# A graph and feed-forward network on one core: where 480 block-table scatters are issued

## The chip, the cores and the metric

The kernel runs on one core of one Trainium2 chip, as one program. The metric is the device time of one execution in microseconds; of the kernel before there are three timed runs, given by their median, and one further execution that was profiled. Engines are named PE (TensorE), DVE (VectorE), ACT (ScalarE), POOL (GpSimd) and SP (SyncE, which here only issues DMAs).

## The reference

Four layers, each a graph step over the same 60,000 edges followed by a feed-forward step over the 3,750 nodes of width 256, each added to the node features `x`:

```
edge_index = jnp.stack([src, dst])
x = x + _L0_gnn_ref(_layernorm(x), ..., src, dst, edge_type_8)
x = x + _L0_ffn_ref(_layernorm(x)[None], ...)[0]
x = x + _L1_gnn_ref(_layernorm(x), ..., edge_index)
x = x + _L1_ffn_ref(_layernorm(x)[None], ...)[0]
x = x + _L2_gnn_ref(_layernorm(x), edge_index, ...)
x = x + _L2_ffn_ref(_layernorm(x)[None], ...)[0]
x = x + _L3_gnn_ref(_layernorm(x), edge_index, ...)
x = x + _L3_ffn_ref(_layernorm(x)[None], ...)[0]
```

The graph steps of layers 0 to 2 are attentions: each edge gets a logit from its two nodes, the logits are put through a softmax over the edges with the same destination, and the source rows are summed with these weights. Layer 3's graph step is a sum over the edges in one direction and back in the other:

```
m = segment_sum(xt[src], dst) * Binv[:, None]
out = segment_sum(m[dst], src) * Dinv[:, None]
```

No number of the result depends on when the block table, of which the change speaks, is written, as long as it is whole before layer 3's blocks are made from it.

## The kernel before

**Staging.** The edges are sorted by destination; the node rows lie in 30 tiles of 128. A program for regular inputs (class `Regular`) runs the phases one after the other: layer 0's features, then `l01` (layers 0 and 1), layer 2, layer 3.

**An attention step** (`Regular.attention`, from line 1844) runs over 75 groups of 7 chunks of 128 edges. For each chunk POOL issues one indirect DMA (`gather`, line 149) that brings 128 rows of the layer's node table from DRAM into the tile `gt`; that makes 525 gathers for a layer. The gathers of group g+1 are issued ahead of the work on group g. PE selects the destination's part of the logits (`ad_ps`, line 1129 in layer 1), DVE adds the gathered part (line 1136), every few groups a softmax over 112 rows is made, and PE sums the weighted rows into `sum_ps` (line 1965). The instructions of DVE, PE, ACT and POOL keep the order in which this loop writes them.

**The node table** of each layer is written just before: in layer 1 (`l1_gnn`, line 1081) for each of the 30 tiles PE multiplies the normed rows with the weights, ACT copies the product (`h`), and SP stores it to DRAM (`l1_h`, line 1111; profile names leave the digits out, so it is `l_h` there). Layer 2 does the same with `l2_vk` (line 1314, `l_vk` in the profile), which its gathers read. A gather waits for all 30 stores of its table. Layer 0's table, `l_feat`, was made earlier, before `l01`.

**The block table.** Layer 3 works with dense blocks of the graph. They are made, during layer 2's feed-forward, from a DRAM table `blocks` that says for every place which edge sits there. It is filled by 480 scatters, each an indirect DMA on POOL (`scatter`, line 154) that writes one four-byte entry for each of 125 rows to a place of its own; the places and entries were worked out beforehand and lie in `put_dram`. The scatters are declared independent of each other.

**Where the scatters are.** `l01` (line 2028) issues them in two trains, each after an attention step has been issued in full and before the feed-forward step of the same layer. POOL works off its queue in order, so a train follows the 525 gathers of its own layer and stands ahead of the gathers of the next. Neither feed-forward step gives POOL any work. The helper `beside` does one train: it reserves the tile `put`, has DVE clear it near the end of the attention (the hook `self.behind`, called when the last group's gathers are out), which keeps the load of `put` from going ahead of its time, loads `put` by a DMA on POOL's queue (line 2047), and issues the scatters one column at a time. The tiles of both trains, `put0` and the second, lie beside each other in one pool, and hold 480 columns between them.

Of the kernel before, what the change touches and what calls it, by code (L numbers as in the profile page):

```python
# [28 lines left out]
EP, EC = 125, 480  # L29
# [29 lines left out]
class Gnn:  # L59
# [938 lines left out]
    def l01(self):  # L998
        self.l0_gnn()
        self.sort_by_src(self.l0_ffn)  # L1000
        self.l1_gnn()
        self.l1_ffn()
# [814 lines left out]
class Regular(Gnn):  # L1817
# [210 lines left out]
    def l01(self):  # L2028


        nc = self.nc
        self.blocks = self.dram.tile([P * NCB, 1], I32, name="blocks")
        with ExitStack() as st:
            with ExitStack() as st2:
                wp, = self.pools(st2, none=1)
                none = wp.tile([P, NCB], I32, name="none")
                nc.gpsimd.memset(none, P)
                nc.sync.dma_start(self.blocks.rearrange("(p k) a -> p (k a)", p=P), none)
            pool, = self.pools(st, put=1)
            group = self.new_group()  # L2040

            def beside(gnn, c0, c1):
                put = pool.tile([EP, 2, c1 - c0], I32, name=f"put{c0}")

                self.behind = lambda: nc.vector.memset(put, 0)
                gnn()
                nc.gpsimd.dma_start(put, self.put_dram[:, :, c0:c1])
                for c in range(c1 - c0):
                    self.scatter(self.blocks, put[:, 0, c:c + 1], put[:, 1, c:c + 1], group)
            beside(self.l0_gnn, 0, 320)  # L2050
            self.l0_ffn()
            beside(self.l1_gnn, 320, EC)
            self.l1_ffn()
            self.behind = None

# [255 lines left out]
```

## Time and profile before

| | |
|---|---|
| timed runs, us | 6545.5, 6604.4, 6623.24 (median 6604.4) |
| the profiled execution's own time, us | 6483.59 |
| its span, us | 6481.8 |
| busy PE, DVE, ACT, POOL, us | 4548.9, 3065.8, 2065.1, 2916.3 |
| mean granted TensorE clock | 0.80 |
| scatters | 480, of 1.17 us at least, 1.18 in the median, 44.98 at most |
| first and last start of a scatter, us | 1185.9, 2792.4 |
| gathers of layer 0, first and last start, us | 366.7, 1157.9 |
| gathers of layer 1 | 525, from 1690.0 to 2482.1 |
| gathers of layer 2 | 525, from 2975.5 to 3875.8 |
| first read of `blocks` | 3906.8 |

All times within the execution are counted from the start of its span. "Busy" counts work on the engine itself; register, branch, semaphore and DMA-issuing instructions aren't in it. For a gather or a scatter on POOL the trace shows the interval in which POOL works on the instruction, with some 0.30 us between one and the next. [...] a line of the profile gives, next to an instruction, how long its engine sat idle before it and what released it; "issue" there means that it waited for nothing that the profile shows.

### The profile page before, as it was taken

What the parts mean: (1) busy time and instruction counts of PE and PEld (TensorE: products, weight loads), DVE (VectorE), ACT (ScalarE), POOL (GpSimd) and SP (SyncE); (2) the same over time, 40 slices, a digit from 0 to 9 for tenths busy, and PEclk for the clock granted to TensorE, in tenths of its full rate; (3) what the DMA queues carried; (4) which work ended last, traced back from release to release, by engine and by line L of the source; (5) the groups of instructions that cost most, each with busy time, mean ns of one, the idle gap of its engine ahead of it and who ended that gap; (6) DMA issues with size and microseconds to landing.
All of it is one profiled execution on the core that took longest, in us unless ns stands there. A gap on an engine that the chain in (4) does not pass through costs nothing. (4 is left out here: it accounts for less than half of the span.)

```text
span 6481.8 us, 64863 instructions
## 1 busy us (share of the span) xinstructions
PE 4548.9 (70%) x20438; PEld 3297.5 (51%) x20438; DVE 3065.8 (47%) x7333; ACT 2065.1 (32%) x4862; POOL 2916.3 (45%) x2845
## 2 busy tenths in 40 slices
PE   6826666695066664896566773798879898896885
PEld 3425555464055553554454662576546565564673
DVE  5634443793033336544566777403532342266435
ACT  1125554322055553322444552222631121110121
POOL 0046666677766666713455650012025445452124
PEclk9957777797577776898777885697589999998896
DMA  4334444102244442114555661222434554455114
GB/s 148 133 97 116 116 117 116 40 2 42 57 114 117 114 118 63 16 47 148 163 169 163 202 199 43 95 85 77 160 126 143 136 133 131 134 147 160 50 55 116
DMA packets 431163, 714.02 MB, mean 110 GB/s; under 512 B 117452, under 2 KB 308628, under 8 KB 426716
## 3 DMA queue, kind: packets, MB, share of 16 engines
q0 software_dynamic: 145136, 379.81, 22.7%
q1 hardware_dynamic: 267064, 316.47, 15.5%
q10 hardware_dynamic: 18612, 13.50, 0.7%
q8 instruction: 166, 2.72, 0.2%
q14 instruction: 185, 1.52, 0.1%
HBM read 583.81 MB, written 125.15 MB: 109 GB/s over the span
## 5 line engine op out<-in xcount | busy, mean ns | idle before, releaser
L1965 PE MATMUL sum_ps<-gt,oh 128*128 128x260 f32 (+2 forms) x3150 | 1016.4, 483 | 355.9 <-issue 187.4
L1965 PEld LDWEIGHTS sum_ps<-gt,oh 128*128 128x128 f32 x3150 | 744.0, 243 | 551.7 <-issue 226.6
L150 POOL DMA_INDIRECT gt<-l_vk,srci x525 | 497.2, 947 | 586.1 <-issue 186.6
L156 POOL DMA_INDIRECT blocks<-put x480 | 644.5, 1343 | 154.1 <-issue 145.7
L150 POOL DMA_INDIRECT gt<-l_feat,g x525 | 501.1, 954 | 304.4 <-issue 242.1
L150 POOL DMA_INDIRECT gt<-l_h,srci x525 | 496.5, 946 | 296.8 <-issue 203.5
L1947 DVE TENSOR_TENSOR gt<-gt,bank 128x1792 f32<-128x1792 f32 x225 | 453.4, 2015 | 111.1 <-issue 60.8
L1839 ACT ACTIVATE oh<-iota,dloc 128x128 f32<-128x128 f32 x1575 | 481.4, 386 | 32.4 <-PE sum_ps L1965 19.5
L150 POOL DMA_INDIRECT gt<-l_mtab,l_idxm x300 | 294.5, 982 | 361.1 <-ACT gt L2170 208.5
L150 POOL DMA_INDIRECT gt<-l_xtab,srci x262 | 254.2, 970 | 389.7 <-DMA l_xtab<-xt 192.6
L2184 PE MATMUL two_ps<-l_twox,slab 128*128 128x512 bf16 x1080 | 370.1, 391 | 26.7 <-issue 26.6
L147 PE MATMUL y_ps<-f_w,hT 128*128 128x256 f32 x1600 | 357.8, 383 | 17.0 <-DVE y L1075 16.8
L2184 PE MATMUL two_ps<-l_twom,slab 128*128 128x512 bf16 x1080 | 359.8, 379 | 0.0
L2184 PEld LDWEIGHTS <-slab 128*128 128x128 bf16 x2160 | 213.4, 99 | 271.8 <-issue 44.4
L147 PEld LDWEIGHTS y_ps<-f_w,hT 128*128 128x128 f32 x1600 | 305.7, 192 | 68.2 <-DVE y L1075 21.7
L2186 PE MATMUL third_ps<-l_thirdx,slab 128*128 128x257 bf16 x1080 | 300.0, 279 | 23.4 <-issue 19.5
L1830 ACT ACTIVATE ohT<-rows,iota_p 128x896 f32<-128x896 bf16 x225 | 235.2, 1045 | 249.1 <-issue 139.3
L2186 PE MATMUL third_ps<-gt,oh 128*128 128x257 f32 x1124 | 273.9, 388 | 35.4 <-DVE oh L2173 29.6
L2186 PE MATMUL third_ps<-l_thirdm,slab 128*128 128x257 bf16 x1080 | 294.8, 273 | 0.0
L1922 ACT ACTIVATE fw<-fw 112x128 f32<-112x128 f32 x76 | 23.5, 309 | 827.6 <-DVE fw L1921 546.9
L1129 PE MATMUL ad_ps<-l_node,ohT 128*128 128x4 f32 x1050 | 151.2, 269 | 187.5 <-DVE l L1136 134.1
L1322 PE MATMUL q_ps<-l_qt,ohT 128*128 128x256 f32 x1050 | 251.6, 393 | 39.9 <-DVE gt L1328 30.3
(544 smaller groups left out, 8689.5 us busy)
## 6 DMA issues: line engine op xcount, KB each, us to landing
rows<-dl_dram SPq DMA_DIRECT2D x225, 224.0 KB
slab<-adT SPq DMA_DIRECT2D x36, 960.0 KB
slab<-ad SPq DMA_DIRECT2D x30, 1152.0 KB
l_feat<-ft SPq DMA_DIRECT2D x30, 1040.0 KB
f_w<-in_L_ffn_w_dram SPq DMA_DIRECT2D x18, 1024.0 KB
adT<-db_rowT SPq DMA_DIRECT2D x36, 480.0 KB
ad<-db_row SPq DMA_DIRECT2D x36, 480.0 KB
f_yt<-y SPq DMA_DIRECT2D x114, 128.0 KB
```

The source lines that it names most:

```text
L147: self.nc.tensor.matmul(ps, xT[:, c, :], w[:, c, :], start=(c == 0), stop=(c == kc - 1))
L150: return self.nc.gpsimd.indirect_dma_start(out=out, out_offset=None, in_=table, in_offset=bass.IndirectOffsetOnAxis(ap=idx, axis=0))
L156: inst = self.nc.gpsimd.indirect_dma_start(out=table, out_offset=bass.IndirectOffsetOnAxis(ap=idx, axis=0), in_=src, in_offset=None)
L1129: nc.tensor.matmul(ps[:, j, :], ohT[:, j * P:(j + 1) * P], node[:, ds(tiles[j], 1), :H].rearrange("p a h -> p (a h)"), start=True, stop=True)
L1322: nc.tensor.matmul(ps[:, j, :], ohT[:, j * P:(j + 1) * P], flat(q[:, ds(tiles[j], 1), :]), start=True, stop=True)
L1830: nc.scalar.activation(t, rows, AF.Abs, bias=self.iota_p, scale=-1.0)
L1839: nc.scalar.activation(oh[:, j, :], self.iota, AF.Abs, bias=self.dloc[:, c + j:c + j + 1], scale=-1.0)
L1922: nc.scalar.activation(fw, fw, AF.Exp)
L1947: nc.vector.tensor_tensor(rows, rows, wj.unsqueeze(3).to_broadcast([P, GC, H, DH]), ALU.mult)
L1965: nc.tensor.matmul(open_[1], oh[:, j, :], gt[:, j, :W], start=starts(k), stop=starts(k + 1))
L2184: nc.tensor.matmul(flat(ps), block, flat(two[n][:, blocks[i][1]]), start=(i == 0), stop=(i == len(blocks) - 1))
L2186: nc.tensor.matmul(ps3[:, :D + 1], block, rhs, start=(i == 0), stop=(i == len(all3) - 1))
```

## The change

The border between the two trains moves from column 320 to column 215. The first train, behind layer 0's attention, then has 215 scatters in place of 320, and the second, behind layer 1's, has 265 in place of 160. Nothing else is edited; which scatters there are, what each writes and the order among them stay as they were.

```
-            beside(self.l0_gnn, 0, 320)
+            beside(self.l0_gnn, 0, 215)
             self.l0_ffn()
-            beside(self.l1_gnn, 320, EC)
+            beside(self.l1_gnn, 215, EC)
             self.l1_ffn()
             self.behind = None
```

`EC` is 480. On the engines' queues the changed program differs in this alone: the column counts of the two `put` tiles, of their clears on DVE and of their loads on POOL, and the place of 105 scatters on POOL, which go from ahead of layer 1's 525 gathers to behind them. PE, ACT and SP issue the same instructions in the same order.

## The prediction

> **What bounds the kernel now.** I began with the page: no engine is busy for more than 70% of the span (PE), and the chain of waits that ended last is only followed back to 3674 us, so it says nothing of layers 0 and 1, where the change lies. I therefore read the scatters themselves (tile `blocks`): 480 of them on POOL, from 1185.9 to 2792.4 us, in two trains. Then the table of stretches, cut at the end of layer 0's feed-forward, at the last store of layer 1's table and at the end of the first train. Its columns are the stretch, its length, busy time of PE, PE weight loads, DVE, ACT and POOL with instruction counts, granted TensorE clock, DMA share and GB/s:
>
> ```profile
> 1520.00:1565.00 45.00, 39.45 (x188) 30.91 (x188) 17.28 (x82) 21.74 (x89) 35.86 (x31) 0.96 0.38 95
> 1565.00:1690.00 125.00, 1.85 (x9) 1.76 (x9) 0.00 (x0) 3.10 (x3) 99.12 (x85) 0.50 0.10 6
> 1690.00:1750.00 60.00, 12.85 (x59) 12.64 (x59) 2.88 (x13) 5.45 (x5) 45.46 (x48) 0.50 0.42 112
> ```
>
> In the middle row only POOL works: 85 scatters, while PE has 1.85 us of work in 125, DVE none. The waits of this part and the timelines around it say who waits for what (start, length, engine, line; in brackets idle before and releaser):
>
> ```profile
> DVE l L1136 <- DMA gt<-l_h,srci: 146.9, 2, 138.2
> ...
> 1532.55 1.18 POOL L156 DMA_INDIRECT blocks<-put  x1 [0.30 <-issue]
> 1534.03 1.18 POOL L156 DMA_INDIRECT blocks<-put  x1 [0.30 <-issue]
> ...
> 1561.93 0.32 SPq L1111 DMA_DIRECT2D l_h<-h  x1
> ...
> 1688.53 1.18 POOL L156 DMA_INDIRECT blocks<-put  x1 [0.30 <-issue]
> 1690.02 1.00 POOL L150 DMA_INDIRECT gt<-l_h,srci  x1 [0.30 <-issue]
> ...
> 1700.59 0.19 DVE L1136 TENSOR_TENSOR l<-ad_ps,gt 128x28 f32<-128x28 f32 x1 [138.23 <-DMA gt<-l_h,srci]
> ```
>
> The table that layer 1 gathers from gets its last store at 1561.93, but the first gather stands in POOL's queue behind the 320th scatter and goes out at 1690.02, with the usual 0.30 us of issue before it: it waited for its turn, not for data. DVE waits 138 us for its rows, and PE and ACT wait for DVE. So the time here is set by POOL's queue. At the other end of layer 1 it is the reverse:
>
> ```profile
> 2792.35 1.18 POOL L156 DMA_INDIRECT blocks<-put  x1 [0.30 <-issue]
> 2975.52 1.05 POOL L150 DMA_INDIRECT gt<-l_vk,srci  x1 [181.99 <-DVE hd_hc L702]
> ```
>
> The second train (160) is over 182 us before layer 2's first gather, which is held by the table: DVE starts the attention's constants at 2974.88, released by the landing of `l_vk`. PE is busy 107.86 of 115 us in the stretch 2860 to 2975, so the wait there is real work.
>
> [...] DVE gets its rows at 1700.59. Hence I count POOL's instruction intervals for the queue, and landings apart. [...] two scatters that ran beside unbroken DVE work on two SBUF inputs and ended with it:
>
> ```profile
> 1211.47 27.85 POOL L156 DMA_INDIRECT blocks<-put  x1 [0.30 <-issue]
> ...
> 2540.35 44.98 POOL L156 DMA_INDIRECT blocks<-put  x1 [0.30 <-issue]
> ```
>
> [...] 0.50 granted in the idle stretch, 0.50 in the start after it. So the idle time saves up no clock that its removal would cost.
>
> **The change part by part.** Nothing is added or removed: 480 scatters, two loads of `put`, two DVE clears of `put` (0.59 and 0.33 us for 640 and 320 columns, which become 430 and 530), and the same total of columns. The order of PE, DVE, ACT and SP is unchanged; on POOL 105 scatters move from ahead of layer 1's 525 gathers to behind them. Each carries one DMA of 125 four-byte rows. No queue but POOL's is crossed, and no wait is added.
>
> *First train.* One scatter takes 1.18 us and 0.30 of issue, 1.483 from start to start. The 105 that leave are 105 x 1.483 = 155.7 us. Counted back from the first gather, 1690.02 - 155.7 = 1534.3; the row at 1534.03 is the 216th, so the new train is over at about 1533.7. Its 27.85 us stall is near its start and stays. The table is not there before its last store lands: for `l_vk` the last store was issued at 2972.7 and the gather began at 2975.52, 2.8 us later. So the first gather goes to 1561.93 + 2.8 = 1564.7, and POOL has then been idle for 31 us. Of the 155.7 us, 31 pay nothing; the gain is 1690.02 - 1564.7 = 125.3. What else must be ready at 1565? The pieces for the first two groups are: PE made their `ad_ps` by 1566.85, DVE its last `l_node` at 1562.19, and the next two `rows` loads went out at 1564.97 and 1567.95, before the first group's rows can land (10.6 us after its first gather, by 1690.02 to 1700.59). I take off 1 us: 124.
>
> *Layer 1's attention* runs from 1690 to 2482 at its own pace: POOL is busy 495.6 of 792 us in it, PE 471.0, ACT 387.8, so none is full and its length does not depend on when it begins. It moves as a whole. So do its end and the feed-forward.
>
> *Second train.* It begins 124 us earlier, at 2507.16 - 124, and is 105 scatters longer. In the old clock these run from 2793.8 on, beside the last 55 us of the feed-forward and the first 100 of layer 2's projections. Pace: the tail of the 160 has 34 in 50 us and 29 in the last 44, so 1.47 to 1.52 each; at 1.50 it is 157.5, ending at 2951.3. Layer 2's first gather is due at 2975.5, so 24 us are spare, and the cost is nothing. Without that cover each further microsecond is lost. The slowest pace that the trace has there, outside the stall, is 1.43 + 0.30 = 1.73; with all 105 at that, 182 us, it ends exactly at 2975.5. Lower bound zero: POOL has nothing else in that gap that could gain. DVE's work there, 0.69 us evictions with about 1 us between, leaves gaps, unlike the 28 and 45 us stretches. DMA: a lone train takes 10% of the engines, the projections' stretch 28%; layer 1's stores ran beside scatters with PE 39.45 of 45 us busy. I put this contention at 0 to 5 us and take 0. `blocks` is read at 3906.8 at the earliest, 950 us after.
>
> *Sum:* -124 + 0. The profiled execution, 6483.6 us (span 6481.8), becomes 6359.6. The median of the runs is 6604.4, 120.8 longer than that execution, and no view shows where. If that were slower matmuls (120.8 of 4548.9 busy us, 2.7%), the 273 us of PE work from 1260 to 1565 (193.00, 40.59 and 39.45 in three stretches) would end 7 us later and the gain be 117. If it sat on POOL (120.8 of 2916.3, 4.1%), the 504 us train would be 21 longer and the gain 145. So 117 to 145, and I keep 124: 6604.4 - 124 = **6480**.
>
> **Rivals.** *The second train overruns in part.* If [...] the projections' DMAs stretch the 105 scatters to 2.0 us, they end at 3003.8, 28 us late, and the gain is 96: 6508. For it: the two stalls, and 1.3 to 1.43 us scatters beside the feed-forward. Against: DVE's gaps, and 31 scatters in 45 us beside the like stage of layer 1.
>
> *Layer 1 doesn't start when its gathers may.* Some load queued on SP behind the table, or a buffer, takes the place of the wait and half of the gain is lost: 62, giving 6542. Against: the first groups' inputs were made by 1567. If the whole idle time came back, at 6604, the change would in effect do nothing.
>
> *Slower.* The second train becomes the bound of layer 2[...]. It decides from 24 us of overrun on, and outweighs the gain from 24 + 124 = 148 us, when the 105 scatters take 2.9 us each in place of 1.5. At 3.3 each: 105 x 1.8 - 24 = 165 lost, 124 won, 6645. For it only the 45 us stall, which would have to come three times over; against it every regular row.
>
> **How the numbers follow.** Chances: forecast 0.80 (117 to 145 gained), a part of the gain 0.11, nothing 0.05, slower 0.04. The runs spread over 78 us, so half of that, 39, goes on either side of the first case: 6604.4 - 145 - 39 = 6420 to 6604.4 - 117 + 39 = 6526. I make it 6410 to 6525, which takes in most of the overrun case and leaves out some 2 in 10. Two per cent, about what a measurement of this kernel can tell from no change, is 132 us, inside 117 to 145: within the first case I put 0.62 beyond it, since the upper bound reaches farther from 124 than the lower. Faster 0.80 x 0.62 + 0.11 x 0.2 = 0.52; slower 0.04; the rest, 0.44, within 2%.
>
> **What would show it.** Right: the first `l_h` gather 3 us after the last store of that table, with POOL idle some 30 us before it; DVE's 138 us wait at L1136 down to some 13; layer 1's attention still about 792 us long; the last scatter some 20 us before layer 2's first gather, which stays released by DVE's constants. Wrong: an `l_vk` gather with only 0.30 us of issue before it right behind a scatter, a third long scatter, or a new wait of tens of microseconds at L1129 or L1136.

## The result and the profile after

| | before | after |
|---|---|---|
| median of 20 timed runs, us | 6573.3 (6538.2 to 6651.3) | 6519.9 (6509.0 to 6540.7) |
| profiled execution, us | 6483.59 | 6525.78 |
| first and last gather of layer 1, us | 1690.0, 2482.1 | 1584.4, 2380.1 |
| last scatter, us | 2792.4 | 2853.4 |
| first and last gather of layer 2, us | 2975.5, 3875.8 | 2874.9, 3900.3 |
| from the last gather of layer 2 to the end, us | 2606.0 | 2623.6 |

The ratio after to before is 0.9947, with a 95% interval of 0.9927 to 0.9966: a gain of 53 us, under half of the 124 forecast, with the median inside the range given, 40 us above the 6480. That it lies inside is luck: the kernel before came out at 6573.3 here and not at the 6604.4 of its first three runs, from which the same gain would have led to 6551. The profiled execution of the kernel before is 55 us shorter than the shortest of its own 20 timed runs, so the two profiles can't be compared in their totals, only part by part.

The stall of layer 1 is gone. The timeline of the changed kernel, for POOL and for SP's stores of the table (start, length, engine, line; in brackets idle before and releaser):

```profile
1549.43 1.18 POOL L156 DMA_INDIRECT blocks<-put  x1 [0.30 <-issue]
...
1579.25 2.29 SPq L1111 DMA_DIRECT2D l_h<-h  x2
...
1584.42 1.00 POOL L150 DMA_INDIRECT gt<-l_h,srci  x1 [33.80 <-issue]
...
2853.41 1.18 POOL L156 DMA_INDIRECT blocks<-put  x1 [0.30 <-issue]
2874.87 1.05 POOL L150 DMA_INDIRECT gt<-l_vk,srci  x1 [20.28 <-DVE hd_hc L702]
```

The first train is over at 1550.6, POOL is idle for 33.8 us, and the gather follows the last store (the second of the row "x2", at 1581.2) by 3.2 us. The stretch between holds work of PE, where the 125 us of the kernel before had 1.85:

```profile
1549.00:1584.00 35.00, 30.17 (x150) 23.78 (x148) 12.47 (x64) 16.50 (x68) 1.31 (x2) 0.98 0.27 90
```

The wait at line 1136 of 138 us has become one of 13.2 at most (waits of the changed kernel within layer 1; total, number, longest):

```profile
DVE l L1136 <- DMA gt<-l_h,srci: 44.4, 5, 13.2
```

Counted from the first scatter, layer 1's gathers begin 122.7 us earlier than before (381.4 for 504.1), and they take 795.7 us for 792.1. The second train ends 20.3 us ahead of layer 2's first gather, which DVE's constants release, as before. Up to there everything is as predicted, and the changed kernel leads by 100.6 us, by 117.7 counted from the first scatter. The lead is lost in **layer 2's attention**, 1025.4 us long for 900.3. The table of stretches, with layer 2's pass of the kernel before cut at 3577, and that of the changed kernel at the same distance from its start (columns as in the prediction):

```profile
2975.50:3577.00 601.50, 354.14 (x1360) 289.69 (x1360) 354.92 (x529) 244.16 (x522) 309.37 (x327) 0.75 0.57 168
3577.00:3875.80 298.80, 229.64 (x886) 184.79 (x887) 235.20 (x345) 166.20 (x373) 186.86 (x198) 0.85 0.69 203
```

```profile
2874.90:3476.00 601.10, 339.96 (x1298) 278.19 (x1298) 338.13 (x501) 232.93 (x498) 296.59 (x313) 0.74 0.56 161
3476.00:3900.30 424.30, 237.85 (x930) 195.08 (x930) 245.21 (x367) 169.91 (x378) 199.98 (x211) 0.74 0.54 153
```

For the first 600 us the two go nearly alike, at 26 to 28 us for a pair of groups. The kernel before then goes over to 20.6 us a pair, within one pair, and keeps it to the end; the changed kernel never does. What stands in the way is seen in the waits over this pass, before and then after:

```profile
DVE al L1929 <- remote: 125.2, 21, 6.9
ACT al L1931 <- issue: 114.1, 30, 6.8
```

```profile
DVE al L1929 <- remote: 259.1, 32, 11.8
ACT al L1931 <- issue: 252.2, 32, 10.9
```

Line 1929 waits for PE's transpose of `fw` (line 1924); the traces of set 2 below name it as the releaser, where these say "remote". At the slow pace DVE, ACT and PE all stand still there, once for nearly every pair. I counted in each trace, from 15 us after the first gather of layer 2's pass to its last, the stretches of over 2 us in which none of PE, DVE and ACT has an instruction running: 127.6 us before, 274.0 after. The difference, 146, is more than the 125 by which the pass is longer.

### The profile page after: what moved, and what is told of

The parts are those of the page before. It is cut to its first block, busy times and chain, and to the rows that moved or that the text cites. A ratio compares the mean times of both kernels' runs of the same rounds, so it can differ in the third digit from the quotient of the medians.

```text
span 6524.0 us, 64749 instructions
## 1 busy us (share of the span) xinstructions
PE 4544.5 (70%) x20324; PEld 3306.5 (51%) x20438; DVE 3068.4 (47%) x7333; ACT 2064.1 (32%) x4862; POOL 2921.8 (45%) x2845
## 5 line engine op out<-in xcount | busy, mean ns | idle before, releaser
L2184 PE MATMUL two_ps<-l_twox,slab 128*128 128x512 bf16 x1026 | 354.8, 391 | 28.1 <-issue 27.8
L2184 PE MATMUL two_ps<-l_twom,slab 128*128 128x512 bf16 x1020 | 341.9, 379 | 0.0
L1976 PE MATMUL bank<-less,at_row 112*128 112x8 f32 (+1 forms) x146 | 41.7, 358 | 317.2 <-issue 156.9
```

The source lines that it names most:

```text
L2184: nc.tensor.matmul(flat(ps), block, flat(two[n][:, blocks[i][1]]), start=(i == 0), stop=(i == len(blocks) - 1))
```

## The experiments

The runs came in five sets; the kernels of a set ran on one chip, beside the kernel before, whose level differs between the sets. Gains are therefore told against the kernel before of the same set; where an expectation gives an absolute time, it was written for the level of the first runs, and its distance to before is what counts.

**Set 1** (before 6482.4, of 9 runs): is the difference in layer 2's pass chance, and has the second train a part in it?

`e1_before_again` is the kernel before, unchanged, in one execution.

> The kernel before, profiled once more, to see how much one execution's layer 2 attention differs from another's. Theory (layer 2's pass has two paces of its own, 20.5 and 26 to 28 us for two groups, and the first profile happened to switch to the quick one two thirds through): the pass from its first to its last gather is unlike the 900 us of the first profile, up to 1000, and the whole execution is between 6538 and 6651 as the timed runs are. Rival (the pass is 900 us long in the kernel before, and the longer second train is what slows it): again within 10 us of 900. Both: layer 1's first gather again about 504 us after the first scatter.

6493.2 us. The pass took 895.3 us, with the quick pace from the 21st pair as in the first profile. That is what the rival said.

`e2_after_again` is the changed kernel, unchanged, in one execution.

> The changed kernel, profiled once more. Theory of two paces: the pass of layer 2 may be anywhere from 870 to 1030 us, and the total follows it one for one. Rival (the second train slows it): again within 10 us of 1025. Both: layer 1's first gather about 3 us after the last store of its table and 381 us after the first scatter.

6454.1 us, 28 us faster. The pass took 981.5 us and never turned quick. The length lies in the range of the theory and outside the 1015 to 1035 of the rival, so these two runs alone don't decide. Layer 1's first gather again came 3.2 us after the last store.

`e3_215_none` leaves the second train out:

```
-            beside(self.l1_gnn, 215, EC)
+            beside(self.l1_gnn, EC, EC)     # here: gnn() alone, no put, no scatters
```

> The changed kernel without its second train: 215 scatters behind layer 0, none behind layer 1, so 265 places of the block table stay unfilled and layer 3 computes with a part of the edges only. Theory of two paces, with no bearing of the scatters on them: layer 2's pass is still 980 to 1030 us in most executions, and the median within 20 us of the changed kernel's 6520. Rival (the second train, ending 20 us before the pass, slows it): the pass falls to about 900 and the median to about 6400.

6364.4 us, ratio 0.983 (0.980 to 0.986): 118 us faster than before. The pass took 914.7 us and turned quick at its 23rd pair. Without its second train, the change gains nearly what was forecast.

`e4_236_244` moves the border to 236.

> Border at 236: the first train is then over about when layer 1's table is there, and the second is 21 scatters, 31 us, shorter than in the changed kernel. Theory of two paces: the stall of layer 1 stays away (first gather at most 5 us after the last store), layer 2's gathers start when their table is there, and the pass takes its own pace: the median within 20 us of 6520. Rival (a second train that ends close to the pass): with 50 us between its end and the pass rather than 20, the pass is shorter than 1025 and the median below 6490.

6433.6 us, 49 us faster, ratio 0.993 (0.991 to 0.995). Layer 1's gathers still start 3.1 us after the last store; the pass took 966 us and stayed slow. That a second train of 244, ending 51 us ahead of the pass, leaves it as slow as one of 265 does (982 us in this set) speaks against its last microseconds as the cause.

**Set 2** (before 5871.4, of 31 runs): each train's length by itself.

`e5_after_timed` is the changed kernel. The three others are splits:

```
e6_320_265:  beside(self.l0_gnn, 0, 320)   beside(self.l1_gnn, 215, EC)
e7_215_160:  beside(self.l0_gnn, 0, 215)   beside(self.l1_gnn, 320, EC)
e8_320_none: beside(self.l0_gnn, 0, 320)   no second train
```

> The changed kernel, timed beside the next three on one chip, with a third profile of it. Theory A (the longer second train, which ends 20 us rather than 180 us before layer 2's pass, is what slows that pass; without it the whole 124 us come through): slower than 215 + 160 by 60 to 100 us, and the pass again 980 to 1025 us without a change to the quick pace of 20.6 us. Theory B (the pace of the pass is chance, whatever the scatters do): the profile may show the quick pace this time, and the median is that of 215 + 160 within 20 us.

> The first train as before (320), the second as in the changed kernel (265), so 105 entries are written twice with the same values: the longer second train alone, with layer 1's stall kept. Theory A: the second train now ends some 20 us before layer 2's first gather, as in the changed kernel; slower than before by 60 to 100 us, layer 2's pass 980 us or more. Theory B: within 20 us of before, since 105 scatters under cover cost nothing.

> The first train as in the changed kernel (215), the second as before (160): 105 places of the block table stay unfilled, and layer 3 computes with a part of the edges only. The stall's removal alone. Theory A: faster than before by 115 to 125 us, as the kernel without any second train was by 118; the pass of layer 2 about 900 us with the quick pace from about its 21st pair of groups. Theory B: anywhere between 30 and 125 us faster, as the changed kernel itself.

> The kernel before without its second train (160 places of the block table unfilled, layer 3 computes with a part of the edges only). Theory A: the 160 scatters end over 180 us ahead of the pass and don't touch it: within 10 us of before. If each second train slowed the pass by its length, wherever it ends, this would be 40 us or more faster. Theory B: within 20 us of before.

On this chip the executions are some 10% shorter (before: 5871.4 us for 6482.4). Theory A fails, and the numbers of theory B are met, but not by the chance that it speaks of: the pass has one pace here in all four. Against before, the changed kernel gained **123.5 us** (5747.9; ratio 0.9786, 0.9769 to 0.9802), the stall's removal alone 120.7 (5750.7), the longer second train alone 0.5 (5870.9), and leaving out the 160 was worth 7.5 (5863.9). Here the sum of the prediction holds, and the second train is free. Layer 2's pass took 713 to 720 us in all four, without one idle stretch over 2 us. The whole pass of `e5_after_timed` as a stretch:

```profile
2558.50:3271.60 713.10, 571.28 (x2239) 466.41 (x2240) 588.41 (x872) 407.08 (x893) 496.45 (x525) 0.84 0.77 227
```

PE and DVE are busy as long as in the profile after (571 for 578 us, 588 for 583); it is the idle time that is gone.

**Set 3** (before 6485.6, of 10 runs): three of these again. By held-up signals the expectations from here on mean such waits as that of `e18_after` in the last section, where DVE goes on only 5.58 us after the start of a transpose of 0.32 us.

> The changed kernel again, timed, since the chip of the last four runs was unlike those before it: there the kernel before took 5871 us and the passes had no stretch over 2 us in which PE, DVE and ACT all do nothing in layer 2, while on the first two chips such stretches [...] made up 128 us of layer 2's pass in the kernel before and 214 to 274 in the changed one. Theory J (the removed stall is worth 124 us everywhere; on a chip with the held-up signals part of it is lost to more of them in layer 2): on a chip of the first kind, with before at 6450 to 6600, 25 to 60 us faster and 200 us or more of idle stretches in layer 2's pass; on one of the other kind 118 to 127 us faster. Theory C (chip alone, the gain is a fixed share): the same ratio of 0.979 on both kinds.

6439.0 us, 47 us faster, ratio 0.991 (0.989 to 0.994). The pass took 978.7 us, 200 of them in idle stretches.

> The longer second train alone, layer 1's stall kept (105 entries are written twice with the same values). On a chip with the held-up signals, theory J with the late end of the second train as what brings on more of them: 50 to 100 us slower than before, layer 2's pass 960 us or more. If the second train has no part in it: within 20 us of before. On a chip without them: the same as before within 10 us, as measured.

Three of four executions took 6555 to 6558 us, 69 to 73 us more than the kernel before, and one took 6382, 104 us less. With executions so far apart no loss can be put on this kernel. The profiled one (6554.6) has a pass of 954 us, without the quick pace. The train had not overrun:

```profile
2956.27 1.18 POOL L156 DMA_INDIRECT blocks<-put  x1 [0.30 <-issue]
2978.03 1.05 POOL L150 DMA_INDIRECT gt<-l_vk,srci  x1 [20.58 <-DVE hd_hc L702]
```

> The stall's removal alone (105 places of the block table unfilled, layer 3 computes with a part of the edges only). On a chip with the held-up signals, theory J with the second train as their cause: 110 to 125 us faster than before, layer 2's pass about 900 us, as without any second train. If it is the earlier start of layer 1 that matters: 25 to 60 us faster, like the changed kernel. On a chip without them: 118 to 127 us faster.

6324.6 us, 161 us faster, ratio 0.971 (0.965 to 0.978): more than expected and more than the stall is worth, since the pass turned quick at its 16th pair and took 857.5 us. It is 114 us less than `e9_after_3`.

So on such a chip the kernel with the 105 scatters more is slower, although POOL issues every one of them under cover. What is left is whether their number or their late end does it.

**Set 4** (before 6595.4, of 39 runs).

`e12_delay_160` and `e13_265_delay` clear a spare tile on POOL, ahead of the second train's scatters or behind them:

```
+                for _ in range(pads[0]):
+                    nc.gpsimd.memset(pad, 0)
                 for c in range(c1 - c0):
                     self.scatter(...)
+                for _ in range(pads[1]):
+                    nc.gpsimd.memset(pad, 0)
```

> 215 scatters behind layer 0; behind layer 1 POOL first clears a spare tile 285 times, some 155 us, and then issues the last 160 scatters (105 places of the block table unfilled, layer 3 computes with a part of the edges only). The short second train, but ending 10 to 30 us ahead of layer 2's pass, as the long one does. Theory E (it is the lateness of the train's end that brings on the held-up signals all through layer 2's pass): on a chip with them the pass is 950 us or more and the kernel some 100 us slower than 215 + 160 without the delay, that is 30 to 70 us faster than before. Theory N (it is the number of scatters): the pass is 860 to 910 us and the kernel 110 to 160 us faster than before. On a chip without held-up signals both say 115 to 125 us faster.

> The changed kernel with 330 such clears behind its second train, so that layer 2's first gather goes out some 180 us after the last scatter, as in the kernel before, though its table is ready some 155 us earlier. The result is the reference's. Theory E: on a chip with held-up signals layer 2's pass is again 860 to 910 us; the kernel then loses 155 and wins back some 80 against the changed one, so it is 20 to 50 us slower than before. Theory N: the pass stays at 970 us or more, and the kernel is some 100 us slower than before. On a chip without them: slower than before by 30 to 40 us.

Both failed as experiments: nothing tied the clears to their place, and POOL made them between the gathers of layer 0, whose pass grew to 856 and 866 us (810 in `e14_al_first` on the same chip). The trains stood where they would have stood without them. `e12_delay_160` took 6453.9 to 6565.2 us (ratio 0.980, 0.968 to 0.992), `e13_265_delay` 6592.7 in the median (ratio 1.000, 0.997 to 1.003): 160 behind layer 1 is better than 265 once more, with 46 and 57 us lost in layer 0. The profile of `e12_delay_160` is of its longest execution (the three others took 6454 to 6492); its pass of 1010 us was quick for four pairs only. The passes of `e13_265_delay` and of the next kernel, 1051 and 1066 us, never were. All three are left out of the table further down.

`e14_al_first` works out `al` ahead of the transpose:

```
-                nc.tensor.transpose(w_ps, fw, self.ident[:RB, :RB])
                 al = None
                 if joins(batch["c0"]):
                     ...
+                nc.tensor.transpose(w_ps, fw, self.ident[:RB, :RB])
```

> The changed kernel with the factor al worked out ahead of the transpose of fw in place of behind it, so that its DVE and ACT work doesn't wait for PE's transpose (the line at which DVE stood for 212 to 259 us in layer 2's pass on the first two chips). If the held-up signals only hit that one wait: up to 150 us faster than the changed kernel on such a chip, that is 120 to 200 us faster than before. If the wait moves to the next reader of the transpose, the scaling of the rows: within 40 us of the changed kernel. On a chip without them: at most 30 us faster than the changed kernel (0.5 us in 100 batches, some of it hidden).

6580.4 us, ratio 1.000 (0.997 to 1.003); the changed kernel itself was not timed on this chip. The wait moved to the next reader of the transpose, line 1947, and is no shorter there (waits over its pass; in `e13_265_delay` DVE waits 268 us for "remote" at line 1929 and 46 at line 1947):

```profile
ACT gt L1948 <- DVE gt L1947: 400.3, 70, 10.8
DVE gt L1947 <- remote: 385.7, 34, 11.6
```

It isn't that one wait, then: whichever instruction is the first to read the transpose waits for it.

**Set 5** (before 6481.6, of 7 runs): the delays with the clears tied in place, and two kernels to compare with.

```
e15_delay_160, ahead of the load of put (160 columns, 256 spare ones):
+                for _ in range(times):          # 180
+                    nc.gpsimd.memset(put, 0)
e16_265_delay, behind the scatters:
+                for _ in range(times):          # 310
+                    nc.gpsimd.memset(put, 0)
```

> The last delayed train again, with the clears tied in place: behind layer 1's attention POOL first clears the (longer) tile put 180 times, some 150 us, then loads it and issues the last 160 scatters, so that these end some 20 us ahead of layer 2's first gather (105 places of the block table unfilled, layer 3 computes with a part of the edges only). Theory E (the late end of the train matters): on a chip with held-up signals layer 2's pass is 950 us or more in most executions, and the kernel like the changed one, 20 to 60 us faster than before. Theory N (the number of scatters matters): like 215 + 160 without the delay, 110 us or more faster than before. On a chip without held-up signals both say 115 to 125 us faster.

> The changed kernel with 310 clears of put behind its second train, tied in place by the scatters' reads of it, so that layer 2's first gather goes out some 180 us after the last scatter and some 155 us after its table is ready. The result is the reference's. Theory E: on a chip with held-up signals the pass is quick at least in part, 860 to 910 us, and the kernel 30 us or more faster than the changed one plus 160. Theory N: the pass stays at 970 us or more, and the kernel is the changed one plus 160 within 20 us. On a chip without held-up signals: slower than before by 25 to 50 us.

> 215 + 160 on the same chip as the two delays (105 places of the block table unfilled, layer 3 computes with a part of the edges only). On a chip with held-up signals: 110 us or more faster than before, as measured once. On one without: 118 to 127 us.

> The changed kernel on the same chip as the two delays. On a chip with held-up signals: 25 to 60 us faster than before, its pass of layer 2 at 970 us or more. On one without: 118 to 127 us faster.

| | us | against before | ratio |
|---|---|---|---|
| `e17_215_160` | 6321.7 | -160 | 0.975 (0.973 to 0.977) |
| `e18_after` | 6444.9 | -37 | 0.994 (0.992 to 0.996) |
| `e15_delay_160` | 6344.0 | -138 | 0.977 (0.975 to 0.980) |
| `e16_265_delay` | 6609.6 | +128 | 1.018 (1.016 to 1.021) |

Of the five executions of `e17_215_160` one took 6418.8 us and the profiled one 6266.8, the others 6313 to 6324; of the four of `e15_delay_160` one took 6441.0, the others 6331 to 6346. So now and then a short second train loses some 100 us too.

The long train with a long pause behind it, the end of the train and the first gather of `e16_265_delay`:

```profile
2834.77 1.18 POOL L156 DMA_INDIRECT blocks<-put  x1 [0.30 <-issue]
3024.48 1.01 POOL L150 DMA_INDIRECT gt<-l_vk,srci  x1 [0.55 <-issue]
```

190 us lie between the two starts, for 183 in the kernel before, and the pass still took 983 us at the slow pace. The kernel is 164.7 us slower than `e18_after`; its first gather was 165.5 us later. The pause bought nothing, though it isn't that of the kernel before in all: POOL clears in it, and PE, DVE and ACT have no instruction at all from 2880 to 3020. The short train with a short pause, `e15_delay_160`:

```profile
2784.79 1.18 POOL L156 DMA_INDIRECT blocks<-put  x1 [0.30 <-issue]
2871.72 1.06 POOL L150 DMA_INDIRECT gt<-l_vk,srci  x1 [85.75 <-DVE hd_hc L702]
```

The clears took 154 us, as planned, but the scatter of 45 to 48 us that most second trains have is missing in this one (the longest takes 27.5), so the train ends 86 us ahead of the pass rather than 20; the pass took 864 us, as quick as that of `e11_215_160_again` with its 179. **With 265 scatters the pass is slow even when they end 188 us ahead of it, so the late end isn't what makes it slow; the number of scatters in the second train remains.** That 160 which end 20 us ahead would leave the pass quick was not shown. The two kernels whose texts differ in 105 scatters alone, `e17_215_160` and then `e18_after`, each with its whole pass as a stretch:

```profile
2860.30:3651.30 791.00, 568.01 (x2230) 457.81 (x2230) 585.00 (x868) 402.22 (x881) 495.79 (x524) 0.85 0.70 205
```

```profile
2858.90:3831.20 972.30, 576.67 (x2230) 472.16 (x2230) 583.13 (x868) 405.29 (x881) 496.70 (x525) 0.75 0.57 166
```

They start within 1.4 us of each other (first column) and have the same work, and one takes 181 us longer. That is the widest case, since the profiled `e17_215_160` was the fastest of its five; the medians are 123 us apart. The unfilled places have no part in it: from the last gather of layer 2 to the end the two take 2613.6 and 2614.6 us. But one thing more differs. The landings of POOL's DMAs are told on eight semaphores (counters by which one part of the chip tells another that it is done) in turn, 111 to 118, and with 375 scatters ahead of it the pass starts on 111, with 480 on 112. The kernel before and the changed one both start on 112, so this can't be what parts them; how much of the 123 us is due to it was not tested.

The profiles of the other sets together, from the traces (us; the third column counts from start to start; pair: the first at the quick pace of some 20.6 us, counted at line 1931, which runs for 37 pairs of groups):

| profile | scatters | from the last scatter to the first gather | pass | idle stretches | pass less these | quick from pair |
|---|---|---|---|---|---|---|
| before | 320 + 160 | 183 | 900 | 128 | 773 | 21 |
| `e1_before_again` | 320 + 160 | 181 | 895 | 132 | 764 | 21 |
| `e3_215_none` | 215 + 0 | | 915 | 142 | 773 | 23 |
| `e11_215_160_again` | 215 + 160 | 179 | 858 | 92 | 766 | 16 |
| `e17_215_160` | 215 + 160 | 179 | 791 | 35 | 757 | 1 |
| `e15_delay_160` | 215 + 160 | 87 | 864 | 90 | 774 | 16 |
| after | 215 + 265 | 21 | 1025 | 274 | 751 | never |
| `e2_after_again` | 215 + 265 | 20 | 982 | 214 | 767 | never |
| `e9_after_3` | 215 + 265 | 22 | 979 | 201 | 778 | never |
| `e18_after` | 215 + 265 | 24 | 972 | 198 | 775 | never |
| `e16_265_delay` | 215 + 265 | 190 | 983 | 196 | 787 | never |
| `e4_236_244` | 236 + 244 | 52 | 966 | 199 | 767 | never |
| `e10_320_265_again` | 320 + 265 | 22 | 954 | 179 | 775 | never |
| set 2, all four | various | various | 713 to 720 | 0 | 713 to 720 | |

Outside set 2, the pass less its idle stretches is 751 to 787 us in every row. So the stretches account for the differences between 791 and 1025 within some 20 us, and the kernels whose second train has 0 or 160 scatters have 142 us of them at most, those with 244 or 265 at least 179. Of the profiles left out one doesn't fit: that of `e12_delay_160`, with 160 and in its longest execution, has 247.

No version with the whole table was found that beats the changed kernel by more than these runs can tell: 236 + 244 gained 49 us where the changed kernel gained 28, 47 and 37.

## Why the prediction was wrong, point by point

**First train and stall: right.** 215 scatters end well ahead of the table; the first gather follows the last store by 3.0 to 3.4 us in the profiles of the changed kernel (2.8 predicted). The term of 124 us is 120.7 (`e7_215_160`) and 123.5 us (`e5_after_timed`) where nothing else moves.

**Layer 1's attention moves as a whole: right.** With 215 or 236 scatters first it took 789 to 802 us in the profile after and in sets 1, 3 and 5, for 792 before.

**Second train: the step that failed.** The prediction put its cost at nothing, since it would end 24 us ahead of layer 2's first gather. It does end 19 to 23 us ahead in the profiles of the changed kernel, and yet the pass behind it takes 972 to 1025 us on the chips outside set 2, where that of the kernel before takes 895 and 900. In sets 1, 3 and 5 the changed kernel gains 28, 47 and 37 us of the 124, so against the kernel before the term of 0 is 77 to 96 us; against 215 + 160 it is 114 (set 3) and 123 us (set 5). With 320 scatters in the first train no number can be given for it (`e10_320_265_again`), and in set 2 it is nothing: 0.5 us with 320 in the first train, and with 215 the longer kernel is even 2.8 us faster (`e7_215_160`, `e5_after_timed`). The working asked only whether POOL and the DMA queues are done in time. It took the pass behind for a block of fixed length, without a reason; yet that pass has two paces on these chips, and which it keeps differs between the two kernels. The profile of before held the hint: its pass changes from 26 to 20.6 us a pair at 3577, with the wait at line 1929 gone, and I had read its length as one number. The case that came, a part of the gain, had been given 0.11.

**The rival of an overrun** had the sign, and its 6508 lies near the 6519.9 only because the base was lower: it forecast a gain of 96 us, and 53 came. Its mechanism was wrong: no train overran, and where the whole pass was moved away from it (`e16_265_delay`) nothing was won back.

**The base.** The profiled execution of 6483.6 lay below all 20 timed runs of its kernel. The prediction bounded that difference as slower matmuls or a slower POOL. Where the difference sits in these 20 runs was not measured. The kernel before took 6458 to 6533 us in sets 1, 3 and 5, and 6539 to 6660 in set 4, so the profile may stem from a chip like the former and the timed runs from one like the latter; no run shows it. Between the chip of set 2 and that of set 1 a gather takes 0.95 us in the middle in both `e5_after_timed` and `e2_after_again`, and two matmuls of line 1965 at the full clock are 0.222 us apart in both. PE is busy 98 us less in the first, of 705 us by which its span is shorter, and DVE, ACT and POOL within 6 us as long; the rest is waiting.

**What the working took from the profile of before.** POOL's work on layer 1's seventh gather ends at 1698.5 us and DVE starts on the rows at 1700.59, 2.1 us later, so landings had to be counted apart from POOL's intervals. Across the two scatters of 27.85 and 44.98 us DVE is busy for 27.82 and 44.88 us, and the changed kernel has two such scatters again, of 27.53 and 48.00 us; that DVE's work is what holds POOL there was my estimate, and no view shows it. The granted clock was 0.50 in the 125 us in which layer 1's start waited and 0.50 in the 60 us after; in the changed kernel it is 0.98 in the 35 us ahead of layer 1's gathers and again 0.50 in the 60 after, so the removal cost no clock there.

**Still open** is by what way 105 more scatters, done before the pass begins, keep it at its slow pace. The order of instructions in layer 2 and the semaphores that they wait for are the same in the kernel before and the changed one, and the total of 480 scatters too. A pause does not undo it. The effect is not one of the second train's length alone either: 215 + 160 turns quick sooner than 320 + 160, and 215 + 0 later than 215 + 160. With one or two profiles of each, some of this may be chance, and the slow executions of the short trains and the one quick execution of `e10_320_265_again` (6382 us) say that no train settles it every time. What tells the two paces apart in a trace is known, and stands in the last section. Spreading the 105 over the gaps of layer 1's pass wasn't tried.

## What to carry to other kernels

The 105 scatters fitted under their cover, and nothing waited for POOL because of them; whether the stage behind such work keeps its length is another question, and a stage that shows two paces within one profile is a warning that it may not. Before a stage's length goes into a sum as a constant, plot its period over time, not its total. And where a gain is missing, test the part on its own (the stall's removal without the work that was moved, the moved work without the stall's removal): here the first of these gained 121 us on one chip and some 160 on two others, where the whole change gained 124, 47 and 37, which no single profile tells.

## What the runs showed of the hardware

**Signals held up in POOL's bursts of gathers.** The timeline of one slow pair in `e18_after`, from the first gather of POOL's burst of 14:

```profile
3443.73 0.94 POOL L150 DMA_INDIRECT gt<-l_vk,srci  x1 [9.72 <-issue]
...
3452.03 0.31 ACT L1922 ACTIVATE fw<-fw 112x128 f32<-112x128 f32 x1 [5.64 <-issue]
3452.39 0.32 PE L1924 MATMUL bank<-ident,fw 112*128 112x112 f32 x1
3452.47 0.95 POOL L150 DMA_INDIRECT gt<-l_vk,srci  x1 [0.30 <-ACT fw L1922]
...
3457.47 0.95 POOL L150 DMA_INDIRECT gt<-l_vk,srci  x1 [0.30 <-issue]
3457.97 0.22 DVE L1929 SCALAR_TENSOR_TENSOR al<-bank,mc,ends_b 112x1 f32<-112x1 f32 x1 [5.98 <-remote]
3458.22 0.20 ACT L1931 ACTIVATE al<-al 112x1 f32<-112x1 f32 x1 [5.89 <-issue]
...
3458.74 0.59 PE L1976 MATMUL bank<-less,at_row 112*128 112x8 f32 x2 [6.03 <-issue]
```

and the same place in `e5_after_timed`:

```profile
2936.80 0.31 ACT L1922 ACTIVATE fw<-fw 112x128 f32<-112x128 f32 x1 [5.38 <-DVE fw L1921]
2937.16 0.31 PE L1924 MATMUL bank<-ident,fw 112*128 112x112 f32 x1
2937.24 0.95 POOL L150 DMA_INDIRECT gt<-l_vk,srci  x1 [0.30 <-ACT fw L1922]
2937.51 0.22 DVE L1929 SCALAR_TENSOR_TENSOR al<-bank,mc,ends_b 112x1 f32<-112x1 f32 x1 [0.75 <-PE bank L1924]
```

The transpose takes 0.32 and 0.31 us. DVE starts 0.35 us after its start in the second, 5.58 us in the first, and once it is done POOL alone of the four engines works until then. The trace shows nothing that DVE waits for still being worked on; I take it that the news of it is late. In those 5.58 us the semaphore events of the first trace, DMA landings most of them, come in small groups some 0.7 us apart (at 3452.99, 3453.67, 3454.40, 3455.09, 3455.80, 3456.66, 3457.20, 3457.91), and some sixty come within 1.5 us once the burst is over, from 3463.55 on. In set 2 such pauses hardly occur: inside the bursts of the whole pass `e5_after_timed` has 13 of over 0.55 us between two events, `e18_after` 539. What holds them up no view shows. On the chips where it happens the trace also lacks many of them: it has 32,146 events of DMA landings in `e18_after` and 74,823 in `e5_after_timed`, the same program. Whether the recording itself has a part in the delay was not tested.

**The place of the transpose in the burst goes with the pace.** The events are spaced like this at the quick pace too. A quick pair of `e17_215_160`:

```profile
3112.83 0.94 POOL L150 DMA_INDIRECT gt<-l_vk,srci  x1 [3.48 <-ACT ohT L1831]
...
3119.57 0.31 PE L1924 MATMUL bank<-ident,fw 112*128 112x112 f32 x1 [0.52 <-issue]
3119.93 0.22 DVE L1929 SCALAR_TENSOR_TENSOR al<-bank,mc,ends_b 112x1 f32<-112x1 f32 x1 [0.75 <-PE bank L1924]
```

In this burst too the events come some 0.7 us apart, from 3118.47 to 3131.78. But the transpose starts 6.7 us after the first gather of the burst, early in that stretch, its own event comes with the group at 3119.90, and DVE goes on 0.36 us after its start; in `e18_after` it starts 8.7 us after the first gather, and DVE goes on 5.58 us later. I took these two times for every transpose of layer 2's pass that falls within 15 us of the start of a burst, in the 15 profiles outside set 2 whose order of instructions is the same (all but `e14_al_first`). Of 109 that start within 7.05 us, 101 let DVE go on within 0.5 us; of the 392 that start after 8.5 us none does within 1.4, and the median is 5.6. Between these bounds both occur. The kernel before and the others that change to the quick pace and keep it do so when one transpose starts 5.1 to 6.1 us into its burst. In set 2 the transposes start at 8.6 us too, and DVE goes on 0.30 us later. So the two paces are two places of the same step in the same burst. What moves the step from one to the other, and what the second train has to do with it, isn't shown.

**The granted clock is lower at the slow pace.** The three stretches of layer 2's whole pass shown above have 568 to 577 us of PE work at a granted clock of 0.84 and 0.85 where it takes 713 and 791 us, and of 0.75 where it takes 972; the kernel before has 0.75 in the slow part of its one pass and 0.85 in the quick part. In the slow pair of `e18_after` above PE stands still for 6.03 us in front of line 1976. Whether such pauses lower the clock, or the lower clock keeps the pace slow, wasn't tried.
